# Layer 1 attention: each transpose of probabilities between two matmuls, its chain two steps later, ten tiles for probabilities

## Chip, cores and metric

The kernel runs on one core of a Trainium2 chip. The metric is the device time of one execution in microseconds, the median of three runs. The profile is of one further execution, taken by the hardware profiler; its instructions carry the line numbers of the kernel.

## What is computed

Two transformer layers on a batch of B = 4 sequences of S = 512 tokens with D = 512 features. Layer 0 is an attention with 32 heads of 16 features that share one key and value head, and a quantized linear layer. Layer 1 is an attention with 32 heads of 128 features over 8 key and value heads, with rotary positions, and a gated FFN with ternary weights. Each of the four parts adds a layer norm of its result to x. The part that the change is about, cut to its core:

```python
q = (hidden_states @ Wq.T).reshape(bsz, q_len, N_HEADS, HEAD_DIM).transpose(0, 2, 1, 3)
...
q = q * cos + _rotate_half(q) * sin
...
k = jnp.repeat(k, GROUPS, axis=1)
v = jnp.repeat(v, GROUPS, axis=1)
scale = 1.0 / jnp.sqrt(jnp.asarray(HEAD_DIM, dt))
scores = jnp.einsum('bhqd,bhkd->bhqk', q, k) * scale
causal = jnp.tril(jnp.ones((q_len, q_len), bool))
scores = jnp.where(causal[None, None], scores, jnp.asarray(-1000000000.0, dt))
attn = jax.nn.softmax(scores, axis=-1)
out = jnp.einsum('bhqk,bhkd->bhqd', attn, v)
out = out.transpose(0, 2, 1, 3).reshape(bsz, q_len, N_HEADS * HEAD_DIM)
return out @ Wo.T
```

All in float32. The shapes in the inputs make q_len 512.

## The kernel before

TensorE works here on operands rounded to a short float32 format. For float32 accuracy each operand is kept as a high and a low half, and a product is three matmuls: high by high, high by low, low by high (`mm3`, L182 to L184). A high half is a ScalarE copy, its low half a VectorE or GpSimd difference.

The program has three stages. Layer 0 and the key and value projections of layer 1 come first and end at about 760 us. Then comes layer 1's attention, `phase_b` (L859 to L1078), and then the FFN (`C.run`, L1169).

`phase_b` goes through 32 units u: 8 groups of four heads times 4 sequences. A unit has four blocks qb of 128 queries, and a block has four heads j. The loop of L1040 makes one step p for each (u, qb, j), so 512 steps and 12 more to drain. With G = p // 4, the number of the block, a step does:

- `score(u, qb, j)` (L954): two or three matmuls of 256 to 512 columns into one of three `psS` banks; VectorE adds the causal mask and finds the row's extreme in one pass (L966, L973); ScalarE takes exp (L977); VectorE a reciprocal (L979); GpSimd scales the row (L980). The result is a tile `s` of the pool `bs`, which has eight.
- `qproj` of the next unit at j = 1 (one head a block), `kproj` at the unit's fourth step: twelve matmuls into one of two `mm` banks, then `rope` (L847): VectorE L850, L852, L853, then GpSimd L854, ScalarE L855, GpSimd L856, through single tiles `rp_a` and `rp_b`.
- `trans(G - 1, kb = j)` (L986), if block G - 1 has a key block j: four transposes on TensorE (L989), one for each head, into one of two `psT` banks; ScalarE copies the bank to `ph` (L992), VectorE makes `pl` (L993).
- `pv` (L996) of the step before: three matmuls (L1002 to L1004) into the single `psO` bank; after the last key block ScalarE and VectorE make `oh` and `ol` (L1008, L1009), which free the bank.
- `oproj(G - 2)` (L1012) at j = 3: twelve matmuls into an `mm` bank, which VectorE adds to `acc`.

Weights come by `load_w` (L892): a DMA on GpSimd's queue into the high half, a second into the single tile `raw`, and a GpSimd difference `w_l` (L902). In the last unit the loop also advances `tail`, the FFN's front for sequence 0 (`C.front`, L1146): layer norms, and four transposes (L147) for each of four blocks of tokens, through one tile each of `x`, `an_t` and `xn` in the pool `cft`.

The order in each engine's queue isn't that of the calls. The framework's scheduler chooses, for every engine, among the instructions whose inputs its own timeline holds ready, and puts in the waits. `issue_after(a)` adds an edge: the instructions of its block come behind `a` on `a`'s engine.

Of the kernel before, what the change touches and what calls it, by code (L numbers as in the profile page):

```python
# [1 line left out]

# [1 line left out]

# [5 lines left out]
F32 = mybir.dt.float32  # L10
# [10 lines left out]
B, S, D = 4, 512, 512  # L21
# [837 lines left out]
def phase_b(tc, nc, c, aps, xt_d, wk_d, v_d, acc, xp, P, tern, tail):  # L859

    if True:
# [21 lines left out]
        nc.sync.dma_start(cosk, aps["c_cosk"])  # L883
        sink = cp.tile([128, S], F32, name="sink")
        nc.sync.dma_start(sink, aps["c_sink"])
        W = {}
        X = {}
        KV = {}
# [41 lines left out]
        def kproj(u):  # L930
            wh, wl = W["k", u // 4]
            xh, xl = X[u]
            ps = mmp.tile([128, S], F32, name="mm", tag="mm")
            mm3(nc, ps, lambda k: wh[:, bass.ts(k, 128)], lambda k: wl[:, bass.ts(k, 128)],
                lambda k: xh[:, k], lambda k: xl[:, k], range(KC))
            k = kvp.tile([128, 2, S], F32R, name="k", tag="k")
            rope(nc, tmp, k[:, 0], k[:, 1], ps, cosk, sink, nc.vector if u < 1 else nc.gpsimd)
            K[u] = k

        def qproj(u, j):  # L940
            h = 4 * (u // 4) + j
            wh, wl = W["q", h]
            xh, xl = X[u]
            ps = mmp.tile([128, S], F32, name="mm", tag="mm")
            mm3(nc, ps, lambda k: wh[:, bass.ts(k, 128)], lambda k: wl[:, bass.ts(k, 128)],
                lambda k: xh[:, k], lambda k: xl[:, k], range(KC))
            qh = qp.tile([128, S], F32R, name="qh", tag="qh")
            ql = qp.tile([128, S], F32R, name="ql", tag="ql")
            rope(nc, tmp, qh, ql, ps, cosq, sinq, nc.vector if u < 1 else nc.gpsimd)
            Q[u, j] = qh, ql  # L950

        PS = {}

        def score(u, qb, j):  # L954
            k = K[u]
            qh, ql = Q[u, j]
            nk = 128 * (qb + 1)
            ps = psS.tile([128, 512], F32, name="ps", tag="ps")
            qs = bass.ts(qb, 128)
            s = sp.tile([128, 512], F32, name="s", tag="s")  # L960
            mn = sm.tile([128, 1], F32, name="mn", tag="mn")
            if qb == 0:
                hl = ps.rearrange("p (i t) -> p i t", i=4)[:, 0:2]
                nc.tensor.matmul(hl, qh[:, qs], k[:, :, :nk], start=True, stop=False)
                nc.tensor.matmul(hl, ql[:, qs], k[:, :, :nk], start=False, stop=True)
                nc.vector.tensor_tensor(s[:, nk:2 * nk], ps[:, nk:2 * nk], c.mask[:, 384:512], ALU.add)  # L966
                mask = s[:, nk:2 * nk]
            else:
                nc.tensor.matmul(ps[:, :nk], qh[:, qs], k[:, 0, :nk], start=True, stop=False)  # L969
                nc.tensor.matmul(ps[:, :nk], qh[:, qs], k[:, 1, :nk], start=False, stop=False)  # L970
                nc.tensor.matmul(ps[:, :nk], ql[:, qs], k[:, 0, :nk], start=False, stop=True)  # L971
# [7 lines left out]
            nc.vector.reciprocal(r, l)  # L979
            nc.gpsimd.tensor_tensor(s[:, :nk], s[:, :nk], r.to_broadcast([128, nk]), ALU.mult)  # L980
            PS[u, qb, j] = s

        O = {}
        PT = {}

        def trans(u, qb, kb):  # L986
            pt = psT.tile([128, 4, 128], F32, name="pt", tag="pt")
            for j in range(4):
                nc.tensor.transpose(pt[:, j], PS[u, qb, j][:, bass.ts(kb, 128)], c.ident)  # L989
            ph = pp.tile([128, 4, 128], F32R, name="ph", tag="ph")  # L990
            pl = pp.tile([128, 4, 128], F32R, name="pl", tag="pl")
            nc.scalar.copy(ph, pt)  # L992
            nc.vector.tensor_tensor(pl, pt, f(ph), ALU.subtract)  # L993
            PT[u, qb, kb] = ph, pl

        def pv(u, qb, kb):  # L996
            vh, vl = KV[u]
            ph, pl = PT.pop((u, qb, kb))
            if kb == 0:
                O[u, qb] = psO.tile([128, 4, 128], F32, name="po", tag="po")  # L1000
            po = O[u, qb]
            nc.tensor.matmul(po, vh[:, kb], ph, start=(kb == 0), stop=False)  # L1002
            nc.tensor.matmul(po, vh[:, kb], pl, start=False, stop=False)  # L1003
            nc.tensor.matmul(po, vl[:, kb], ph, start=False, stop=(kb == qb))  # L1004
            if kb == qb:
                oh = op.tile([128, 4, 128], F32R, name="oh", tag="oh")
                ol = op.tile([128, 4, 128], F32R, name="ol", tag="ol")
                nc.scalar.copy(oh, po)  # L1008
                nc.vector.tensor_tensor(ol, po, f(oh), ALU.subtract)  # L1009
                O[u, qb] = oh, ol  # L1010

        def oproj(u, qb):  # L1012
            g, b = u // 4, u % 4
            oh, ol = O.pop((u, qb))
            y = mmp.tile([128, D], F32, name="mm", tag="mm")
            mm3(nc, y, lambda j: oh[:, j], lambda j: ol[:, j],
                lambda j: W["o", 4 * g + j][0], lambda j: W["o", 4 * g + j][1], range(4))
# [118 lines left out]
class C:  # L1136


    def __init__(self, tc, nc, c, aps, acc, x2_d, m_d, sc, out, xp, P):
        self.nc, self.c, self.acc, self.x2_d, self.m_d, self.sc, self.out = nc, c, acc, x2_d, m_d, sc, out  # L1140
        self.xp = xp
        self.ft = P(name="cft", bufs=1, side="right")
        self.sm = P(name="csm", bufs=3, side="right")
        self.X = {}

    def front(self, b):  # L1146
        mmp = self.c.mmp
        nc, c, sm = self.nc, self.c, self.sm
        xh = self.xp.tile([128, KC, S], F32R, name="xh", tag="xh")
        xl = self.xp.tile([128, KC, S], F32R, name="xl", tag="xl")  # L1150
        bank = Bank(mmp, "mm", Tok(1))
        for t in range(4):
            x = self.ft.tile([128, D], F32, name="x", tag="x")
            nc.sync.dma_start(x, self.x2_d[bass.ts(b * 4 + t, 128), :])
            a = self.acc[:, b * 4 + t]
            rs, nm = yield from ln_gen(nc, c, sm, a)
            tt = self.ft.tile([128, D], F32, name="an_t", tag="an_t")
# [4 lines left out]
            xn = self.ft.tile([128, D], F32, name="xn", tag="xn")  # L1162
            ln_apply(nc, xn, a, rs, nm)
            yield from hop(1)
            ts = bass.ts(t, 128)
# [80 lines left out]
def mega(tc, nc, aps, out):  # L1246
    with ExitStack() as top:
# [34 lines left out]
        with ExitStack() as e3:  # L1282
# [3 lines left out]
            pc = C(tc, nc, c, aps, acc, x2_d, m_d, sc, out, xp, P3)  # L1286
            with ExitStack() as eb:
                phase_b(tc, nc, c, aps, xt_d, wk_d, v_d, acc, xp, pools(eb), tern,
                        pc.front(0))
            with ExitStack() as ec:  # L1290
                pc.run(pools(ec))

# [94 lines left out]
```

## Time and profile before

| | |
|---|---|
| three runs | 2447.71, 2447.67, 2446.82 us; median 2447.67 |
| profiled execution | 2450.93 us, of which the span of its instructions is 2449.2 |
| TensorE matmul busy | 2314.0 us, 94% of the span |
| TensorE weight loads | 1801.1 us, 74%, beside matmuls |
| VectorE, GpSimd, ScalarE | 1574.3, 1202.1, 1075.2 us |
| DMA | 242.60 MB, mean 99 GB/s |
| L989, transposes of probabilities | 1280, 272 ns each in the mean, 212.6 us busy |
| L980, scaling on GpSimd | 512, 723 ns, 360.1 us busy |
| L992 and L993, `ph` and `pl` | 320 each, 586 and 686 ns |

Two things help to read it. Matmuls are pipelined: a matmul of 512 columns is recorded with some 0.39 us, but the next starts 0.23 us after it, so TensorE's pace is read from start to start and not from durations. And idle time of an engine that isn't the bottleneck costs nothing.

### The profile page before, as it was taken

To read this page: it belongs to the slowest core of one execution; us is meant where nothing else is said; L and a number is where in the kernel's file an instruction comes from. 1 tells how busy PE (TensorE), PEld (TensorE's weight loads), DVE (VectorE), ACT (ScalarE), POOL (GpSimd) and SP (SyncE) were. 2 spreads that over 40 slices of the span, in tenths; PEclk is the share of its full clock that TensorE was granted. 3 is DMA by queue.
4 is the path that set the end of the run, shared out by engine and by line. 5 is a ranking of instruction groups with operands and counts; after the bars stand their busy time and mean duration, and the time that the engine had idled before them with its cause. 6 is when DMAs were issued, how large, how long until landed. Compare 5 with 4: busy or idle time off the path is not lost.

```text
span 2449.2 us, 35859 instructions
## 1 busy us (share of the span) xinstructions
PE 2314.0 (94%) x11606; PEld 1801.1 (74%) x11606; DVE 1574.3 (64%) x4631; ACT 1075.2 (44%) x2400; POOL 1202.1 (49%) x1403
## 2 busy tenths in 40 slices
PE   6799889989976999999999999999999999999998
PEld 4566455655554788888888888888888888878887
DVE  7666566555343766777677677777767768764543
ACT  3555445445521444444444444444444445453332
POOL 3332333333342565666566566566666666631220
PEclk9899899999988999999999999999999999999999
DMA  8745434331338543231231232222232222042100
GB/s 180 234 145 177 97 88 109 98 104 60 106 104 237 128 134 104 78 117 58 78 124 63 97 104 91 74 87 104 76 103 72 84 98 74 18 102 75 34 27 18
DMA packets 155295, 242.60 MB, mean 99 GB/s; under 512 B 26802, under 2 KB 87474, under 8 KB 146276
## 3 DMA queue, kind: packets, MB, share of 16 engines
q1 hardware_dynamic: 136948, 199.27, 27.1%
q0 software_dynamic: 16304, 40.12, 5.8%
q8 instruction: 93, 1.52, 0.3%
q10 hardware_dynamic: 1856, 0.92, 0.2%
q14 instruction: 94, 0.77, 0.1%
HBM read 184.22 MB, written 63.92 MB: 101 GB/s over the span
## 4 chain that ended last, share of the span: by engine, by line
PE 82%; DMA 5%; issue 4%; DVE 3%; ACT 2%; POOL 2%; SPq 1%; ACTq 0%; POOLq 0%; DVEq 0%
PE mm L182 10%; PE mm L184 10%; PE mm L183 10%; PE pt L989 5%; PE mm L159 3%; PE po L482 3%; PE pt L466 3%; PE mm L161 3%; PE po L1003 3%; PE po L1002 3%; PE po L1004 3%; PE mm L160 3%; PE ps L969 3%; PE ps L971 3%; PE ps L970 3%
## 5 line engine op out<-in xcount | busy, mean ns | idle before, releaser
L980 POOL TENSOR_TENSOR s<-s,r 128x384 f32<-128x384 f32 (+3 forms) x512 | 360.1, 723 | 119.9 <-DVE r L979 110.4
L977 ACT ACTIVATE s<-s,mn 128x384 f32<-128x384 f32 (+3 forms) x512 | 286.0, 560 | 231.7 <-DVE mn L973 226.8
L854 POOL TENSOR_TENSOR rp_a<-rp_a,rp_b 128x512 f32<-128x512 f32 x155 | 200.7, 1295 | 273.4 <-DVE rp_b L853 264.4
L992 ACT CAST ph<-pt 128x512 fp32r<-128x512 f32 x320 | 181.9, 586 | 295.1 <-PE pt L989 292.7
L429 DVE CUSTOM_DVE_ANT_0 jk<-ps,mask 128x384 bf16<-128x384 f32 (+3 forms) x512 | 227.3, 483 | 82.0 <-PE ps L425 73.1
L993 DVE TENSOR_TENSOR pl<-pt,ph 128x512 fp32r<-128x512 f32 x320 | 216.4, 686 | 38.4 <-ACT ph L992 35.6
L973 DVE CUSTOM_DVE_ANT_0 s<-ps,mask 128x384 f32<-128x384 f32 (+2 forms) x384 | 203.1, 552 | 39.0 <-PE ps L971 19.1
L989 PE MATMUL pt<-ident,s 128*128 128x128 f32 x1280 | 212.6, 272 | 10.1 <-POOL s L980 9.9
L469 ACT ACTIVATE pe<-pt 128x512 f32<-128x512 f32 x307 | 174.6, 600 | 99.8 <-PE pt L466 95.7
L182 PE MATMUL mm<-xh,w_h 128*128 128x512 f32 x512 | 206.6, 403 | 5.5 <-DVE rp_b L853 5.5
L182 PE MATMUL mm<-w_h,oh 128*128 128x512 f32 x512 | 204.3, 399 | 2.6 <-DVE rp_b L853 1.9
L989 PEld LDWEIGHTS pt<-ident,s 128*128 128x128 f32 x1280 | 164.3, 140 | 55.3 <-POOL s L980 10.1
L184 PE MATMUL mm<-xh,w_l 128*128 128x512 f32 x512 | 204.4, 399 | 0.0
L183 PE MATMUL mm<-xl,w_h 128*128 128x512 f32 x512 | 202.9, 396 | 0.0
L183 PE MATMUL mm<-w_l,oh 128*128 128x512 f32 x512 | 202.0, 395 | 0.0
L184 PE MATMUL mm<-w_h,ol 128*128 128x512 f32 x512 | 201.0, 393 | 0.0
L856 POOL TENSOR_TENSOR ql<-rp_a,qh 128x512 fp32r<-128x512 f32 x124 | 160.6, 1295 | 45.2 <-ACT qh L855 45.1
L471 POOL TENSOR_SCALAR_AFFINE_SELECT pe<-pe 128x512 f32<-128x512 f32 x128 | 81.9, 642 | 200.1 <-ACT pe L469 198.7
L850 DVE TENSOR_TENSOR rp_a<-mm,cosq 128x512 f32<-128x512 f32 x128 | 88.4, 690 | 116.6 <-PE mm L184 87.3
L425 PE MATMUL ps<-KS,QS 128*128 128x256 f32 (+2 forms) x384 | 132.9, 384 | 19.2 <-DVE mn L429 18.6
L108 POOL TENSOR_TENSOR ln_rs<-ln_ve,mhalf 128x1 f32<-128x1 f32 x112 | 63.9, 577 | 169.7 <-DVE ln_ve L106 152.2
L1008 ACT CAST oh<-po 128x512 fp32r<-128x512 f32 x128 | 74.5, 582 | 154.8 <-PE po L1004 154.7
(338 smaller groups left out, 5896.9 us busy)
## 6 DMA issues: line engine op xcount, KB each, us to landing
xh<-xt SPq DMA_DIRECT2D x32, 1024.0 KB
xl<-xt SPq DMA_DIRECT2D x32, 1024.0 KB
v<-e_h SPq DMA_DIRECT2D x32, 256.0 KB
v<-e_l SPq DMA_DIRECT2D x32, 256.0 KB
raw<-in_a_wq SPq DMA_DIRECT2D x32, 256.0 KB
vh<-v SPq DMA_DIRECT2D x32, 256.0 KB
vl<-v SPq DMA_DIRECT2D x32, 256.0 KB
w_h<-in_a_wo POOLq DMA_DIRECT2D x32, 256.0 KB, 3.1
```

The source lines that it names most:

```text
L182: nc.tensor.matmul(ps, lh(k), rh(k), start=(j == 0), stop=False)
L183: nc.tensor.matmul(ps, lh(k), rl(k), start=False, stop=False)
L184: nc.tensor.matmul(ps, ll(k), rh(k), start=False, stop=(j == n - 1))
L429: nc.vector.tensor_tensor_reduce(out=jk[:, :nk], in0=p, in1=self.c.mask[:, 384 - 128 * qb:512], scale=-1.0, scalar=3e38, op0=ALU.add, op1= ...
L469: nc.scalar.activation(e, ps, AF.Exp)
L854: eng.tensor_tensor(a, a, r, ALU.add)
L973: nc.vector.tensor_tensor_reduce(out=s[:, :nk], in0=ps[:, :nk], in1=mask, scale=-1.0, scalar=3e38, op0=ALU.add, op1=ALU.min, accum_out=mn)
L977: nc.scalar.activation(s[:, :nk], s[:, :nk], AF.Exp, bias=mn, scale=-1.0, accum_out=l)
L980: nc.gpsimd.tensor_tensor(s[:, :nk], s[:, :nk], r.to_broadcast([128, nk]), ALU.mult)
L989: nc.tensor.transpose(pt[:, j], PS[u, qb, j][:, bass.ts(kb, 128)], c.ident)
L992: nc.scalar.copy(ph, pt)
L993: nc.vector.tensor_tensor(pl, pt, f(ph), ALU.subtract)
```

## The change

- `trans` issues nothing itself any more. It puts its four transposes into a list `pend`. All matmuls of `phase_b` go through `mm`, which issues its matmul behind the transpose that was issued last (`behind`), and then one transpose from the list behind that matmul. So as long as the list holds transposes, a matmul and a transpose take turns, and edges hold them in that order; where it is empty there are no edges. With the fourth transpose `split_p` makes `ph` and `pl`. `pv` empties the list first if its `ph` and `pl` aren't there yet.
- `trans` is called ahead of `score` in its step, and two steps later (`LAG = 2`); `pv` and `oproj` follow it. The loop has two steps more.
- The pool `bs` has ten tiles instead of eight. The pool `cft` goes from beside `phase_b`; the FFN's front for sequence 0 takes its tiles from `bs`, and the later fronts from a pool of three tiles that the FFN opens.

```diff
-        sp = P(name="bs", bufs=8)
+        sp = P(name="bs", bufs=10)
...
+        pend = []
+        behind = []
+        def tick():
+            if pend:
+                behind[:] = [pend.pop(0)()]
+        def mm(*a, **k):
+            with tc.issue_after(behind.pop().ins) if behind else nullcontext():
+                ins = nc.tensor.matmul(*a, **k)
+            if pend:
+                with tc.issue_after(ins.ins):
+                    tick()
...
         def trans(u, qb, kb):
             pt = psT.tile([128, 4, 128], F32, name="pt", tag="pt")
-            for j in range(4):
-                nc.tensor.transpose(pt[:, j], PS[u, qb, j][:, bass.ts(kb, 128)], c.ident)
+            def one(j):
+                ins = nc.tensor.transpose(pt[:, j], PS[u, qb, j][:, bass.ts(kb, 128)], c.ident)
+                if j == 3:
+                    split_p(u, qb, kb, pt)
+                return ins
+            pend.extend(partial(one, j) for j in range(4))
+        def split_p(u, qb, kb, pt):
             ph = pp.tile([128, 4, 128], F32R, name="ph", tag="ph")
...
         def pv(u, qb, kb):
             vh, vl = KV[u]
+            while (u, qb, kb) not in PT:
+                tick()
             ph, pl = PT.pop((u, qb, kb))
...
+        LAG = 2
...
-        for p in range(NU * 16 + 12):
+        for p in range(NU * 16 + 12 + LAG):
             G, j = p // 4, p % 4
             u, qb = G // 4, G % 4
+            G1, j1 = (p - LAG) // 4 - 1, (p - LAG) % 4
...
-                    tg = tail
+                    tg = tail.front(0, sp)
                 next(tg, None)
+            todo, pvq = pvq, []
+            if 0 <= G1 < NU * 4 and j1 <= G1 % 4:
+                trans(G1 // 4, G1 % 4, j1)
+                pvq.append((G1 // 4, G1 % 4, j1))
             if u < NU:
                 score(u, qb, j)
...
-            todo, pvq = pvq, []
-            G1 = G - 1
-            if 0 <= G1 < NU * 4 and j <= G1 % 4:
-                trans(G1 // 4, G1 % 4, j)
-                pvq.append((G1 // 4, G1 % 4, j))
             for t in todo:
                 pv(*t)
-            G2 = G - 2
-            if j == 3 and 0 <= G2 < NU * 4:
+            G2 = G1 - 1
+            if j1 == 3 and 0 <= G2 < NU * 4:
                 oproj(G2 // 4, G2 % 4)
...
-        self.ft = P(name="cft", bufs=1, side="right")
...
-    def front(self, b):
+    def front(self, b, pool):
+        new = lambda name: pool.tile([128, D], F32, name=name, tag="s")
...
-            x = self.ft.tile([128, D], F32, name="x", tag="x")
+            x = new("x")
...
+        ftp = P(name="cft", bufs=3)
...
-            fr = self.front(b + 1) if b + 1 < B else iter(())
+            fr = self.front(b + 1, ftp) if b + 1 < B else iter(())
```

All other matmuls of `phase_b` are rewritten from `nc.tensor.matmul` and `mm3(nc, ...)` to `mm` and a local `mm3` that calls it, with the same operands in the same order.

More of the change, by code (lines that the diff above doesn't have):

```diff
@@ L1 @@
 from contextlib import ExitStack, nullcontext
+from functools import partial
 import numpy as np
@@ L885, in phase_b, with mm3 @@
         nc.sync.dma_start(sink, aps["c_sink"])
+        pend = []
[9 more added lines that the diff above has]
+                    tick()
+        def mm3(ps, lh, ll, rh, rl, ks):
+            n = len(ks)
+            for j, k in enumerate(ks):
+                mm(ps, lh(k), rh(k), start=(j == 0), stop=False)
+                mm(ps, lh(k), rl(k), start=False, stop=False)
+                mm(ps, ll(k), rh(k), start=False, stop=(j == n - 1))
         W = {}
@@ L963, in score @@
                 hl = ps.rearrange("p (i t) -> p i t", i=4)[:, 0:2]
-                nc.tensor.matmul(hl, qh[:, qs], k[:, :, :nk], start=True, stop=False)
-                nc.tensor.matmul(hl, ql[:, qs], k[:, :, :nk], start=False, stop=True)
+                mm(hl, qh[:, qs], k[:, :, :nk], start=True, stop=False)
+                mm(hl, ql[:, qs], k[:, :, :nk], start=False, stop=True)
                 nc.vector.tensor_tensor(s[:, nk:2 * nk], ps[:, nk:2 * nk], c.mask[:, 384:512], ALU.add)
@@ L968, in score @@
             else:
-                nc.tensor.matmul(ps[:, :nk], qh[:, qs], k[:, 0, :nk], start=True, stop=False)
-                nc.tensor.matmul(ps[:, :nk], qh[:, qs], k[:, 1, :nk], start=False, stop=False)
-                nc.tensor.matmul(ps[:, :nk], ql[:, qs], k[:, 0, :nk], start=False, stop=True)
+                mm(ps[:, :nk], qh[:, qs], k[:, 0, :nk], start=True, stop=False)
+                mm(ps[:, :nk], qh[:, qs], k[:, 1, :nk], start=False, stop=False)
+                mm(ps[:, :nk], ql[:, qs], k[:, 0, :nk], start=False, stop=True)
                 mask = c.mask[:, 384 - 128 * qb:512]
@@ L1001, in pv @@
             po = O[u, qb]
-            nc.tensor.matmul(po, vh[:, kb], ph, start=(kb == 0), stop=False)
-            nc.tensor.matmul(po, vh[:, kb], pl, start=False, stop=False)
-            nc.tensor.matmul(po, vl[:, kb], ph, start=False, stop=(kb == qb))
+            mm(po, vh[:, kb], ph, start=(kb == 0), stop=False)
+            mm(po, vh[:, kb], pl, start=False, stop=False)
+            mm(po, vl[:, kb], ph, start=False, stop=(kb == qb))
             if kb == qb:
@@ L1015, in oproj @@
             y = mmp.tile([128, D], F32, name="mm", tag="mm")
-            mm3(nc, y, lambda j: oh[:, j], lambda j: ol[:, j],
+            mm3(y, lambda j: oh[:, j], lambda j: ol[:, j],
                 lambda j: W["o", 4 * g + j][0], lambda j: W["o", 4 * g + j][1], range(4))
@@ L1156, in front @@
             rs, nm = yield from ln_gen(nc, c, sm, a)
-            tt = self.ft.tile([128, D], F32, name="an_t", tag="an_t")
+            tt = new("an_t")
             nc.scalar.activation(tt, a, AF.Identity, bias=nm, scale=rs)
@@ L1161, in front @@
             rs, nm = yield from ln_gen(nc, c, sm, a)
-            xn = self.ft.tile([128, D], F32, name="xn", tag="xn")
+            xn = new("xn")
             ln_apply(nc, xn, a, rs, nm)
@@ L1288, in mega @@
                 phase_b(tc, nc, c, aps, xt_d, wk_d, v_d, acc, xp, pools(eb), tern,
-                        pc.front(0))
+                        pc)
             with ExitStack() as ec:
```

4 lines of the change are left out of this document (2 added, 2 removed).

## Prediction

> **What bounds the kernel now.** I read the page's 40 slices first, then busy time by stretch (columns: TensorE, its weight loads, VectorE, ScalarE, GpSimd, clock), then the instructions in order of time.
>
> ```profile
> PE   6799889989976999999999999999999999999998
> ...
> POOL 3332333333342565666566566566666666631220
> PEclk9899899999988999999999999999999999999999
> ```
>
> ```profile
> 1200.00:1400.00 200.00, 200.00 (x1018) 167.16 (x1017) 143.69 (x387) 89.99 (x231) 125.13 (x137) 1.00 0.25 82
> ```
>
> Layer 1's attention runs from about 763 to 2190 us. After its first 60 us TensorE is busy without a break at full clock, while VectorE has 144 of 200 us, ScalarE 90 and GpSimd 125. A busy TensorE can still hide a short wait, because its matmuls overlap, so I added up start-to-start times. Between 830 and 2100 us a 512-column matmul takes 231 ns from its start to the next one's, 384 columns 175, 256 columns 118. With those and 110 ns per transpose, the sum of the work and the trace's clock drift apart by 2.1 us at 888 us (a wait for a free `mm` bank) and by some 1.5 us in all the rest. So the middle has no waits to win. What is left to win is at its start: from 780 to 823 us the trace falls 18.6 us behind the sum. The tail, 2100 to 2194, falls 6.4 behind.
>
> **1. What a lone transpose costs.** The timeline of TensorE (start and duration in us, engine, line, operation; in brackets the idle time before and what ended it) has both shapes, a run of four and single ones:
>
> ```profile
> 1200.23 0.60 PE L989 MATMUL pt<-ident,s 128*128 128x128 f32 x4
> 1200.59 0.37 PE L970 MATMUL ps<-k,qh 128*128 128x256 f32 x1
> 1200.79 0.40 PE L1002 MATMUL po<-ph,vh 128*128 128x512 f32 x1
> ...
> 1205.27 0.27 PE L989 MATMUL pt<-ident,s 128*128 128x128 f32 x1
> 1205.29 0.42 PE L969 MATMUL ps<-k,qh 128*128 128x384 f32 x1
> 1205.55 0.34 PE L970 MATMUL ps<-k,qh 128*128 128x384 f32 x1
> 1205.73 0.34 PE L971 MATMUL ps<-k,ql 128*128 128x384 f32 x1
> ```
>
> The lone transpose is left after 20 ns, but the matmul behind it then takes 1205.55 - 1205.29 = 260 ns where an undisturbed one of 384 columns takes 175. Together that is 105 to 112 ns. The four take 1200.79 - 1200.23 = 560 ns less the 118 of the matmul that follows: 442, or 110 each. Over 830 to 2100 us the 77 lone ones cost 111.8 ns on average, the 164 runs of four 110.5 each, and no length of run is cheaper than 109. Where one matmul stood between two lone transposes (7 cases), it was 114.3. So whoever comes after a transpose pays for a weight load that 128 columns can't cover, be it the next transpose or a matmul. In the changed program's order 1270 of 1280 transposes stand alone (before: 448 runs). I take 112.5 against 110.4: 1280 x 2.1 ns = **+2.7 us**; the ends are 0 and 3.9 x 1280 = 5 us.
>
> [...]
>
> **2. Waits that the order brings in.** Each transpose now hangs on the matmul before it, and the next matmul on it, so the scheduler can no longer put ready matmuls between a group's last transpose and its use. The chain behind a transpose is: ScalarE's copy `ph`, VectorE's `pl`, then the matmuls of L1002 to L1004. At the end of the layer the trace shows it bare:
>
> ```profile
> 2181.77 0.60 PE L989 MATMUL pt<-ident,s 128*128 128x128 f32 x4
> ...
> 2182.46 0.59 ACT L992 CAST ph<-pt 128x512 fp32r<-128x512 f32 x1 [1.37 <-PE pt L989]
> ...
> 2183.70 0.67 DVE L993 TENSOR_TENSOR pl<-pt,ph 128x512 fp32r<-128x512 f32 x1
> ...
> 2184.42 0.50 PE L1003 MATMUL po<-pl,vh 128*128 128x512 f32 x1 [0.82 <-DVE pl L993]
> ```
>
> TensorE starts 0.05 us after `pl` ends (2183.70 + 0.67 = 2184.37). In the middle of the layer, from the start of a group's last transpose, `ph` ends after 0.90 us at the least (median 1.12), `pl` after 1.62 (lower quartile 1.85, median 2.47). Against that I hold the work that the two programs put on TensorE between that transpose and its users, in the durations above. Before, the least is 2.41 us to the user of `ph` and 3.00 to that of `pl`, and no wait is seen. After, the order repeats from head group to head group, and:
>
> - At 30 places (about one in each of 32 units of four heads) `pl` has 1.72 to 1.84 us. Needed are 1.67 with both engines free, 1.90 at the quartile, 2.52 at the median: a wait of 0, 0.2 or 0.8. VectorE's queue at this place holds one small mask addition of a score (0.29 us) just ahead of `pl`. Laying the rows' durations end to end in queue order, `pl` ends 0.05 to 0.4 us late. I take 0.2: 30 x 0.2 = **+6 us** (0 to 24).
> - At 6 places, in the units that also load new weights, `ph` has 0.34 us and needs 0.95: 6 x 0.65 = **+3.9 us** (2 to 5).
> - At 7 places a score's bank is wanted again after 1.15 us. At 1.57 the trace shows no wait; I take 0 (up to 5, at 0.7 each, one 0.68 reduction of a score being in the way).
>
> Behind a waiting matmul stands all of TensorE, whose idleness is the layer's time; the other engines catch up meanwhile, so waits don't add to each other's price.
>
> **3. The start of the layer.** Here the lag of two steps and ten tiles work:
>
> ```profile
> 784.46 0.28 PE L965 MATMUL ps<-k,ql 128*128 128x256 f32 x1
> 794.68 0.47 PE L989 MATMUL pt<-ident,s 128*128 128x128 f32 x1 [9.94 <-POOL s L980]
> ```
>
> ```profile
> 801.45 1.31 POOL L902 TENSOR_TENSOR w_l<-raw,w_h 128x512 fp32r<-128x512 f32 x1 [6.46 <-DMA raw<-in_a_wo]
> 803.46 0.40 POOL L980 TENSOR_TENSOR s<-s,r 128x128 f32<-128x128 f32 x1 [0.70 <-DVE r L979]
> 805.51 1.30 POOL L854 TENSOR_TENSOR rp_a<-rp_a,rp_b 128x512 f32<-128x512 f32 x1 [1.65 <-DVE rp_b L853]
> ```
>
> The first transpose holds TensorE for 10.2 us, since GpSimd's queue has four `w_l` differences ahead of the scaled scores, each behind a DMA into the single `raw` tile. The clock then falls: the next matmuls take 427 ns, 2.6 us lost in all. After the change the first transpose stands behind 12.9 us of work instead of 3.3, so this wait goes. What is late next? GpSimd keeps its order, and its fourth `w_l` still ends at 801.45 + 1.31 = 802.76. Behind it are one scaling (0.40) and the first rope addition of unit 1, then at about 803.2 where it was 805.51. Every following projection needs an `mm` bank, which a rope frees, and ropes go one after another through the single `rp_a`: VectorE 2.07, GpSimd 1.30, ScalarE 0.62, GpSimd 1.30. The last big wait of the start before (819.78 to 822.23, for VectorE's `rp_b`) is the end of that chain, so it moves by the 2.3 us that the chain starts earlier, and the 10 us are mostly given back there. I take **-2 us**; the ends are 0 and -12.8 (10.2 + 2.6).
>
> **4. The tail.** The two extra steps put the last transposes and the last four L1002 to L1004 groups closer together. `po` has one bank: before, 2.01 us of other work lay between its last two owners (0.43 us of wait); after, 0.23, where the copy `oh` (0.58), `ol` (0.69) and 0.25 of drain must pass. About 1.3 of wait replaces 0.43: **+1 us** (-2, if the front of the FFN gains by its shared tiles, to +3).
>
> **The rest.** The FFN's front for batch 0 takes its three tiles from the ten of the scores, and the later ones from a pool of three in place of three of one each: the same rotation, hidden under the FFN's matmuls; 0 (up to 2 where a score waits for a tile). Output projections move by two steps; their `oh`, `ol` and bank come in time by the order (1.2 us at the least before, 2.2 after). Loads are issued at the same steps on SP's and GpSimd's queues. In layer 0, which no edit touches, the scheduler also gives another order of the same matmuls (1043 of 2916 positions). TensorE idles 120 of the first 800 us; I let a thirtieth of that go either way: 0, +-4 us.
>
> **Sum:** 2.7 + 6 + 3.9 + 0 - 2 + 1 + 0 = +11.6 us. The profiled execution took 2450.93 (span 2449.2 and 1.7 around it), so 2462.5; against the median of the three runs, 2447.67, which is 3.3 lower, it is **2459**. About 0.2%, 4.9 us, is what a measurement of this kernel can tell from no change.
>
> **Rivals.**
> - *The new waits vanish* (25%): ScalarE and VectorE are free at the 30 places and `pl` comes in 1.67. What remains is 2.7 + 3.9 - 2 + 1 = +5.6, or +1.7 without the six: 2449 to 2453. For it: no wait in the middle before. Against: 1.62 is the least of 314 groups, and half of them take over 2.47.
> - *Faster by the start* (15%): the wait for GpSimd at 784 is 12.8 us with its slow clock. If the fourth `raw` lands earlier than 801 us, or the scheduler's order lets ropes pass, the 12.8 stay won: 2447.67 - 12.8 + 2.7 + 1 = 2439, with the waits of part 2 gone, 2443 with the six left. It decides as soon as those cost less than some 4 us. Against: the rope chain above.
> - *The median, not the quartile* (13%): queues at the 30 places are as full as usual, 0.8 each: 24 + 3.9 + 2.7 + 1.4 + 1 - 2 = +31, 2479.
> [...]
>
> **How the numbers follow.** The forecast has 46%, with 2453 to 2468 as its own range. Faster: 15 + 1 = 16%. Within 0.2%: 25%. Slower: 46 + 13 = 59%. The range reaches down to 2440, so that half of the fast case is in, and up to 2475, below the median case: some 80%.
>
> **What would show it.** Right: lone transposes at 110 to 114 ns with the next matmul's; in the waits of TensorE a row of some 10 us for `pl` and `ph`, in equal steps from 870 to 2130 us; the first transpose without its wait, but waits for `rp_b` up to 820. Wrong: no idle TensorE in the middle; the layer's first unit done 10 us sooner; or a matmul behind a lone transpose at its undisturbed time.

## The result and the profile after

The changed kernel takes 2477.47 us in the median of four runs (2474.38 to 2480.60), the kernel before 2447.69 beside it: a ratio of 1.0122 (95% interval 1.0105 to 1.0140). It is 29.8 us slower; I had forecast 11 and a range that ends at 2475. Measured once more in another session, the same program took 2472.76 us, a ratio of 1.0110 (1.0094 to 1.0126). The profiled execution took 2479.49 us, with a span of 2477.8.

The 40 slices of the page show nothing of it, and the table of busy times for 1200 to 1400 us shows little (columns as before):

```profile
PE   6799889989976999999999999999999999999998
...
POOL 3323333333442665665665666565665656522220
PEclk8899999999988999999999999999999999999999
```

```profile
1200.00:1400.00 200.00, 197.96 (x996) 163.04 (x995) 143.84 (x381) 92.05 (x230) 124.58 (x136) 1.00 0.25 80
```

TensorE was busy for all of the 200 us before and is for 197.96 now, with some twenty matmuls fewer. The waits of TensorE from 870 to 2130 us (what waited, for which engine's tile; us in all, times, longest) name the waits that are long enough to leave it idle:

```profile
PE pt L1015 <- POOL s L1005: 6.7, 6, 1.6
PE po L899 <- ACT ph L1025: 3.0, 6, 0.5
PE mm L899 <- DVE rp_b L854: 2.7, 1, 2.7
PE po L899 <- DVE pl L1026: 0.2, 1, 0.2
```

The `ph` row was in the forecast, the first one wasn't, and of a row for `pl` there is next to nothing.

To see where each microsecond went I take, as in the prediction, the clock's time less the sum of the work, with the same durations (231, 175.5 and 118.5 ns for matmuls of 512, 384 and 256 columns, 110 for a transpose), from the layer's first score on. All kernels below have the same work, 1383.5 us up to the FFN's first matmul, so the same marks can be put in each: 68, 150 and 1310 us of work, which is about 860, 945 and 2100 to 2145 us of the clock. "Behind" is what a stretch takes more than its work.

| kernel | median us | ratio (95%) | first score at | behind: start, to 68 | 68 to 150 | middle, 150 to 1310 | tail |
|---|---|---|---|---|---|---|---|
| before | 2447.67 | 1 | 780.0 | 19.1 | 2.3 | 1.3 | 5.8 |
| changed | 2477.47 | 1.0122 | 778.7 | 16.4 | 5.5 | 22.1 | 14.9 |
| after_again: changed, once more | 2472.76 | 1.0110 (1.0094-1.0126) | 772.2 | 18.2 | 2.9 | 22.4 | 15.0 |
| e1_together: no turns | 2436.29 | 0.9960 (0.9945-0.9975) | 771.9 | 16.8 | 2.0 | 0.9 | 3.0 |
| e1_confirm: the same again | 2438.19 | 0.9964 (0.9951-0.9977) | 769.7 | 16.8 | 1.0 | 1.0 | 2.9 |
| e6_no_edges: turns, no edges | 2441.90 | 0.9982 (0.9972-0.9993) | 772.9 | 17.0 | 4.9 | 2.7 | 3.5 |
| e2_tiles_only: before, ten tiles | 2442.18 | 0.9984 (0.9971-0.9996) | 772.4 | 15.8 | 1.1 | 2.6 | 4.4 |
| e3_lag0: turns without the lag | 2493.18 | 1.0184 (1.0165-1.0204) | 776.3 | 17.3 | 4.4 | 35.7 | 17.8 |
| e4_tail_together: no turns in the last unit | 2464.65 | 1.0075 (1.0057-1.0094) | 774.3 | 16.6 | 7.0 | 20.8 | 6.2 |
| f2_spread_wl: output weights spread | 2467.73 | 1.0088 (1.0072-1.0104) | 777.4 | 17.2 | 2.2 | 13.3 | 14.5 |
| f3_pv_later: `pv` a step later | 2456.74 | 1.0042 (1.0027-1.0058) | 773.8 | 21.6 | 0.9 | 4.1 | 11.6 |
| e5_raw2: two `raw` tiles | 2469.97 | 1.0098 (1.0082-1.0114) | 776.1 | 9.6 | 17.7 | 8.8 | 15.1 |
| e7_together_raw2: no turns, two `raw` | 2446.54 | 0.9997 (0.9987-1.0008) | 778.0 | 13.7 | 10.8 | 0.7 | 2.9 |
| f1_together_late_wl | 2443.02 | 0.9983 (0.9974-0.9993) | 775.4 | 23.9 | 0.0 | 1.5 | 2.9 |

Profiles are of one execution each, so a row's stretches needn't add up to its median (e2_tiles_only's profiled execution took 2438.10, e1_confirm's 2433.26). The kernel before had medians of 2446.2 to 2446.4 beside the later ones. The first score, whose code ahead no edit touches, comes at 778.7 and at 772.2 us for one and the same program: some 7 us of any single comparison are not the change's. So stretches are compared from the first score on.

Between the two profiles of the first session the sum closes: first score -1.3, start -2.7, 68 to 150 +3.2, middle +20.8, tail +9.1, FFN -0.6: +28.5, and the spans differ by 28.6. **The loss is made in the middle and in the tail.**

**The middle, +20.8.** At six places, in the units that load new weights, a transpose waits for a score that GpSimd hasn't scaled yet. TensorE at one of them (start, duration, operation; idle time before and its cause in brackets), and GpSimd at the same time:

```profile
1279.57 0.28 PE L899 MATMUL ps<-k,qh 128*128 128x256 f32 x1
1281.40 0.33 PE L1015 MATMUL pt<-ident,s 128*128 128x128 f32 x1 [1.55 <-POOL s L1005]
```

```profile
1272.58 1.30 POOL L927 TENSOR_TENSOR w_l<-raw,w_h 128x512 fp32r<-128x512 f32 x1 [0.43 <-PE ps L899]
1277.83 1.29 POOL L927 TENSOR_TENSOR w_l<-raw,w_h 128x512 fp32r<-128x512 f32 x1 [3.95 <-DMA raw<-in_a_wo]
1279.08 1.27 POOL L855 TENSOR_TENSOR rp_a<-rp_a,rp_b 128x512 f32<-128x512 f32 x1
1280.31 1.75 POOL L1005 TENSOR_TENSOR s<-s,r 128x512 f32<-128x512 f32 x3
```

The second `w_l` waits 3.95 us for its load, because the one `raw` tile is free only when the first `w_l` has read it, at 1273.88; SP's queue issues the load just then:

```profile
1273.90 5.58 SPq L925 DMA_DIRECT2D raw<-in_a_wo  x2
```

Three scalings stand behind the second `w_l`. In the kernel before GpSimd does the same work here in another order, with three scalings ahead of the `w_l`:

```profile
1274.56 1.12 POOL L980 TENSOR_TENSOR s<-s,r 128x128 f32<-128x128 f32 x3 [1.10 <-DVE r L979]
1275.75 1.30 POOL L902 TENSOR_TENSOR w_l<-raw,w_h 128x512 fp32r<-128x512 f32 x1
```

From start to start the six waits cost 7.6 us (0.26 to 1.71 each), and the restarts behind them 1.0 more. At six other places `ph` is late; TensorE shows 0.49 idle, and 0.66 from start to start, 3.95 in all and 0.75 for the restarts:

```profile
1009.52 0.48 PE L899 MATMUL po<-ph,vl 128*128 128x512 f32 x1
1010.49 0.50 PE L899 MATMUL po<-ph,vh 128*128 128x512 f32 x1 [0.49 <-ACT ph L1025]
```

At 27 places, one in nearly every unit, `pl` comes just in time for the matmul, but not for its weight load. TensorE's weight loads at one of them:

```profile
971.54 0.19 PEld L899 LDWEIGHTS po<-pl,vh 128*128 128x128 f32 x1 [0.26 <-DVE pl L1026]
971.65 0.19 PEld L899 LDWEIGHTS po<-ph,vl 128*128 128x128 f32 x1
```

The load of the waiting matmul shows 0.26 us of idle time put down to `pl`, though the 128x128 that it reads are of `vh`. `pl` ends at 971.49, and load and matmul both start at 971.54; the load ahead of it starts at 971.08, 0.24 us before its matmul at 971.32. The next matmul starts at 971.88, after 0.34 us instead of 0.23. That is 0.10 at each, 2.8 us in all, and no idle time is shown. Two further waits for `pl`, at 2079 and 2081 us, are 0.8 together. Waits above 45 ns come to 16.8 us (before: 0.5). The other 4.5 us of the 20.8 lie in pieces below 45 ns. A kernel below that has the lone transposes and almost no waits shows 3.0 us of this; what the remaining 1.5 are isn't shown.

**The tail, +9.1.** TensorE just before the layer's end:

```profile
2200.53 0.39 PE L899 MATMUL po<-ph,vl 128*128 128x512 f32 x1
2202.32 0.80 PE L899 MATMUL po<-ph,vh 128*128 128x512 f32 x1 [1.40 <-DVE ol L1044]
...
2204.20 0.63 PE L1015 MATMUL pt<-ident,s 128*128 128x128 f32 x2
2205.55 0.80 PE L899 MATMUL po<-ph,vh 128*128 128x512 f32 x1 [0.73 <-ACT ph L1025]
```

The wait for the single `po` bank is there as forecast (1.56 us from start to start, through `oh` and `ol`). What is new is that the last groups' transposes, with edges between them and the few matmuls that are left, have nothing to stand before the user of `ph`: 1.12 us twice. And the matmuls take 0.80 where they took 0.39: the granted clock was 0.51 from 2202 to 2212 us. By my estimate that costs some 3.6 us: 11 matmuls at 0.43 us instead of 0.23, a twelfth at 0.39, and 12 transposes at 0.21 instead of 0.11. The kernel before has such a stretch too, from 2186.3 to 2189.7 us, with a granted clock of 0.50, where a matmul takes 0.43 us from start to start instead of 0.23. It costs some 1.5, estimated from the 3.36 us between 2186.45 and 2189.81 less 1.83 of work (six matmuls at 231 ns, four transposes at 110):

```profile
2185.83 0.50 PE L182 MATMUL mm<-w_h,oh 128*128 128x512 f32 x1 [0.68 <-ACT oh L1008]
...
2188.16 0.63 PE L183 MATMUL mm<-w_l,oh 128*128 128x512 f32 x1
2188.59 0.63 PE L184 MATMUL mm<-w_h,ol 128*128 128x512 f32 x1
```

So some 2 of the 9.1 us are a slower clock by these two estimates, and nearly all the rest is waits.

In the changed kernel the granted clock falls from 1.00 to 0.50 at 2202.2 us, 1.28 us into the gap of 1.40, and 1.8 of the 3.0 us up to there, from the first gap's start at 2199.18, were idle. In the kernel before it falls to 0.50 at 2186.3, the longest gap ahead of the fall is 0.82 us, and 1.5 of the 2.7 us from that gap's start at 2183.60 were idle.

### The profile page after: what moved, and what is told of

Read it like the earlier page. It is cut to its first block, busy times and chain, and to the rows that moved or that the text cites. A ratio compares the mean times of both kernels' runs of the same rounds, so it can differ in the third digit from the quotient of the medians.

```text
span 2477.8 us, 35648 instructions
## 1 busy us (share of the span) xinstructions
PE 2330.3 (94%) x11606; PEld 1793.9 (72%) x11606; DVE 1597.6 (64%) x4631; ACT 1097.5 (44%) x2400; POOL 1201.5 (48%) x1403
## 4 chain that ended last, share of the span: by engine, by line
PE 80%; DMA 5%; DVE 5%; issue 4%; ACT 2%; POOL 2%; SPq 2%; ACTq 0%; POOLq 0%; DVEq 0%
PE mm L899 30%; PE ps L899 9%; PE po L899 9%; PE pt L1015 5%; PE mm L160 3%; PE po L483 3%; PE pt L467 3%; PE mm L162 3%; PE mm L161 3%; PE ps L426 3%; PE gu L1238 3%; PE gu L1239 3%; SPq L1166 1%; PE mm L1256 1%; PE mm L1257 1%
## 5 line engine op out<-in xcount | busy, mean ns | idle before, releaser
L1015 PE MATMUL pt<-ident,s 128*128 128x128 f32 x1280 | 336.5, 273 | 9.6 <-POOL s L1005 9.5
L1025 ACT CAST ph<-pt 128x512 fp32r<-128x512 f32 x320 | 187.3, 586 | 323.5 <-PE pt L1015 321.3
L899 PE MATMUL ps<-k,qh 128*128 128x256 f32 (+2 forms) x896 | 277.3, 364 | 0.0
L998 DVE CUSTOM_DVE_ANT_0 s<-ps,mask 128x384 f32<-128x384 f32 (+2 forms) x384 | 209.5, 553 | 52.8 <-PE ps L899 50.3
L1015 PEld LDWEIGHTS pt<-ident,s 128*128 128x128 f32 x1280 | 180.0, 141 | 28.6 <-POOL s L1005 11.7
L899 PEld LDWEIGHTS ps<-k,qh 128*128 128x128 f32 x896 | 163.5, 189 | 35.8
L899 PE MATMUL ps<-k,ql 128*128 128x256 f32 (+2 forms) x512 | 187.7, 375 | 0.0
L856 ACT CAST qh<-rp_a 128x512 fp32r<-128x512 f32 x128 | 79.3, 620 | 215.9 <-POOL rp_a L855 193.5
```

The costliest lines, as they stand in the source:

```text
L899: ins = nc.tensor.matmul(*a, **k)
L998: nc.vector.tensor_tensor_reduce(out=s[:, :nk], in0=ps[:, :nk], in1=mask, scale=-1.0, scalar=3e38, op0=ALU.add, op1=ALU.min, accum_out=mn)
L1015: ins = nc.tensor.transpose(pt[:, j], PS[u, qb, j][:, bass.ts(kb, 128)], c.ident)
```

## The experiments

Main theory after the result: turns held by edges forbid the scheduler to fill between a group's transposes and their users, and they shift GpSimd's order; lag and tiles do no harm. Rivals: the lag itself; the tiles and the front; lone transposes as such; the single `raw` tile.

**e1_together**: all of the change but the turns.

```diff
-            pend.extend(partial(one, j) for j in range(4))
+            for j in range(4):
+                one(j)
```

> The changed kernel with its lag of two steps and its ten tiles, but a group's four transposes issued at once and no edges. Main theory (the order with a matmul between transposes brings the new waits in the middle, 16.8 us, and 8.2 in the tail, while lag and tiles help the start by 2.7): the waits on GpSimd's scaling, on ph and pl in the middle go, the tail falls back to some 7 us, the start gain stays; 2440 to 2449 us. Rival 1 (the lag itself costs: two steps more at the end and a GpSimd that is behind whatever the order of transposes): 2455 to 2470, with the six waits on GpSimd still there. Rival 2 (ten tiles and the shared front cost): above 2455, and the second kernel of this batch, which has only these, slower too.

2436.29 us, 0.9960 (0.9945 to 0.9975): faster than both kernels, and 4 us below the range that I gave. The middle falls from 22.1 to 0.9 behind and the tail to 3.0, below the 5.8 of the kernel before. Rival 1 falls: the two extra steps don't lengthen the end. Against the changed kernel on the same first score (771.9 and 772.2) turns and edges cost 58.5 - 22.7 = 35.8 us; the medians differ by 36.5. The start's wait for GpSimd is still there, 9.0 us at the first transpose, though lag and tiles are those of the changed kernel:

```profile
PE pt L1015 <- POOL s L1005: 10.8, 3, 9.0
```

In TensorE's order 3.2 us of work stand ahead of that transpose, as in the kernel before, and 12.9 in the changed one (9.3 in e3_lag0 below, which has turns and edges without the lag). So turns and edges moved it; the lag alone moves nothing there.

**e2_tiles_only**: the kernel before with ten tiles and the front's tiles taken from them, LAG and turns left out.

> The kernel before with ten tiles in place of eight and the front's tiles taken from them; transposes, lag and order of calls as before. Main theory: tiles neither help nor harm much, 2443 to 2451 us, the first transpose still waits for GpSimd's scaling with some 10 us. Rival 2 (tiles or the shared front cost): above 2455, with scores or the front waiting for tiles. Rival 3 (the start gain comes from the tiles and not from the lag): the wait of 9.9 us shrinks below 5.

2442.18 us, 0.9984 (0.9971 to 0.9996). Rival 2 falls. The wait of the first transpose is 8.9 us as expected, so rival 3 falls too by the sign that I gave it. But the start is 15.8 behind with tiles alone, 3.3 less than in the kernel before, so it isn't shown that the start's gain needs the lag. How much of the gain in the first kernel is the lag's and how much the tiles', I can't say: their intervals overlap, and in the stretches they differ by 1 to 2 us.

**e4_tail_together**: the changed kernel, with no turns in the last unit.

```diff
+            if u == NU - 1:
+                while pend:
+                    tick()
+                for j in range(4):
+                    one(j)
+                return
```

> The changed kernel, but in the last of the 32 units each group's four transposes are issued at once, so that the tail has the order of the kernel before with two steps more. Main theory (the tail's 8.2 us come from the turn-taking there: waits on ph, oh and ol behind edges, and the half clock that follows them): 2469 to 2473 us, the offset of the tail back to some 7 us, no slice at half clock after 2202 us. Rival 1 (the two extra steps themselves): the tail stays within 2 us of 14.9, 2476 to 2480.

2464.65 us, 8.1 below the changed kernel of the later session, and 4 below the range that I gave, which started from the first session's 2477. The tail goes from 15.0 to 6.2 behind; the granted clock is 1.00 from 2190 to 2208 us. The turns and their edges make the tail's loss.

**e5_raw2**: the changed kernel with two `raw` tiles.

```diff
-        raws = P(name="braw", bufs=1)
+        raws = P(name="braw", bufs=2)
```

> The changed kernel with two tiles in place of one for raw, the landing place of a weight's second copy, and nothing else. Theory: the six waits of TensorE on GpSimd's scaling (7.6 us, about 1 us more behind them) come from a w_l difference that waits for its DMA at the head of GpSimd's queue (3.95 us at 1277 us), because the one raw tile lets the next DMA start only when the difference before it is done; with two tiles the DMA is early and these waits go: 2462 to 2469 us, and the start (three such waits before 802 us) a few us shorter. Rival (GpSimd is late at these units from work and not from the DMA, or the DMA is late for another reason): the six waits stay within a third, 2474 to 2480.

2469.97 us, 1 us above the range. In the middle the theory holds: no wait for GpSimd is left, waits above 45 ns fall from 17.0 to 3.9 us (the ones for `ph` go too, since the order moves), and the start is 9.6 behind instead of 18.2. But one new wait of 12.3 us at 902 takes most of it back. GpSimd's queue and SP's around it:

```profile
892.44 1.60 POOL L1005 TENSOR_TENSOR s<-s,r 128x384 f32<-128x384 f32 x2
912.50 1.26 POOL L927 TENSOR_TENSOR w_l<-raw,w_h 128x512 fp32r<-128x512 f32 x1 [18.45 <-DMA raw<-in_a_wo]
```

```profile
902.25 7.40 SPq L1166 DMA_DIRECT2D m_d<-t_d  x10
909.75 0.43 SPq L925 DMA_DIRECT2D raw<-in_a_wo  x1
```

GpSimd stands 18.45 us at a `w_l` whose load is issued only at 909.75, behind ten copies of the FFN's weights (`m_d<-t_d`) on SP's queue.

**after_again**: the changed kernel unaltered.

> The changed kernel once more, unaltered, so that it stands on the same chip as the other kernels of this batch. Its first measurement (2474.4 to 2480.6 in four runs, ratio 1.0122) and the variants of the first batch came from different chips' sessions, and the first score of the layer began at 778.7 us there and at 771.9 to 776.1 in the variants. If layer 0 is only the chip's clock, the first score comes at 772 to 776 here and the ratio is 1.009 to 1.012; if it is the order of layer 0, it stays at 778 to 779 and the ratio at 1.0122. In the middle (950 to 2130 us) the same 16 to 18 us of waits are expected either way.

2472.76 us; the first score at 772.2 us, so its late place wasn't the program's. Whether it was the session's or the single execution's, one profile of each can't tell. Middle and tail come out within 0.3 us of the first profile.

**e3_lag0**: the changed kernel with `LAG = 0`.

> The changed kernel with its edges, single transposes and ten tiles, but without the lag (LAG = 0). Theory: the lag is what the turn-taking order needs, because a block's scaled scores must be there when its transposes are at the head of TensorE's queue; without it the least work between a score and its transpose falls from some 12 to 7.6 us, and waits on GpSimd's scaling come in every unit: 2485 to 2530 us, with over 15 us of waits on GpSimd in the middle. Rival (the lag does nothing in the middle, only ph and pl count): within 8 us of the changed kernel.

2493.18 us, 1.0184 (1.0165 to 1.0204); the middle is 35.7 behind. The waits of TensorE from 950 to 2095 us have one large row:

```profile
PE pt L1015 <- POOL s L1005: 13.7, 29, 0.8
```

That is idle time; from start to start the waits come to 31.4 us, 24 of them ahead of a transpose. So the lag saves the turns some 20 us (2493.18 - 2472.76): it hides VectorE, ScalarE and GpSimd between score and transpose. The lag covers part of what the turns cost.

**e6_no_edges**: turns in the calls, no edges.

```diff
-            with tc.issue_after(behind.pop().ins) if behind else nullcontext():
-                ins = nc.tensor.matmul(*a, **k)
-            if pend:
-                with tc.issue_after(ins.ins):
-                    tick()
+            nc.tensor.matmul(*a, **k)
+            tick()
```

> The changed kernel with the calls in turns (a transpose called after every matmul) but without the edges, so that the scheduler may put ready matmuls in between; runs of single transposes are 393 and of four 104 in its order, and ph has at least 1.49 us of work before its user, pl 4.96. Main theory (the edges, which forbid to fill, cause the waits on ph, pl and GpSimd, not the single transposes as such): middle waits under 3 us, 2437 to 2448 us. Rival (calling transposes one by one is enough to bring the waits): over 10 us of waits in the middle, 2462 to 2480.

2441.90 us, 0.9982 (0.9972 to 0.9993); 1.1 us of waits in the middle. The edges alone account for 58.5 - 28.1 = 30.4 us of the changed kernel's time. The scheduler, left free, regroups the transposes (in the middle 343 of 1064 stand alone, in the changed kernel all) and fills.

**f2_spread_wl**: the changed kernel, each output-weight load in a block of its own, its `w_l` behind a scaling.

```diff
-                if p % 16 == 12:
-                    for jj in range(4):
-                        load_w("o", u // 4 + 1, jj)
+                if p % 4 == 0:
+                    load_w("o", u // 4 + 1, qb)
...
+            with tc.issue_after(SC[0].ins) if which == "o" and SC else nullcontext():
+                eng.tensor_tensor(wl, raw, f(wh), ALU.subtract)
...
+            SC[:] = [nc.gpsimd.tensor_tensor(s[:, :nk], s[:, :nk], r.to_broadcast([128, nk]), ALU.mult)]
```

> The changed kernel with its edges on TensorE, and the loads of output weights spread: in the units that load weights one head's load in each block instead of four at one step, and each w_l held by an edge behind a scaling of its time on GpSimd's queue. Nothing on TensorE is changed. Theory: the six waits of TensorE on GpSimd's scaling (7.8 us on this chip, 1.1 us more behind them) come from two w_l that stand ahead of the scalings on GpSimd's queue while their loads into the one raw tile land; spread, each load has a block's time and these waits go: 2462 to 2467 us, middle waits from 17.0 to 7 to 9. Rival (GpSimd has too much to do at these units however it is ordered): the six waits stay above 5 us, 2469 to 2475.

2467.73 us, 0.7 above the range, with a first score 5 us later than in after_again. The waits in the middle are 8.2 us (expected 7 to 9), the six for GpSimd are gone, `ph` and `pl` stay within 0.05 us. GpSimd at the unit shown above:

```profile
1277.46 0.40 POOL L1007 TENSOR_TENSOR s<-s,r 128x128 f32<-128x128 f32 x1 [0.21 <-DVE r L1006]
1278.22 0.40 POOL L1007 TENSOR_TENSOR s<-s,r 128x128 f32<-128x128 f32 x1 [0.36 <-DVE r L1006]
1278.58 1.29 POOL L929 TENSOR_TENSOR w_l<-raw,w_h 128x512 fp32r<-128x512 f32 x1
```

The scalings pass, and the `w_l` finds its load there. TensorE's order is that of the changed kernel up to each of the six waiting transposes; behind each, one score matmul moves by 17 places. So the six waits were GpSimd's queue and nothing else.

**f3_pv_later**: the changed kernel with `pv` a step later, four tiles of `ph` and `pl`, and nine of the probabilities, as they need the room.

```diff
-            todo, pvq = pvq, []
+            todo, pvq, pvq2 = pvq2, [], pvq
```

> The changed kernel with its edges, but pv a step later, so that more work lies between a group's last transpose and the users of ph and pl; ph and pl get four tiles each instead of three, and to fit them the probabilities nine instead of ten. By the order the least work ahead of ph's user goes from 0.23 to 1.39 us, and ahead of pl's from 1.61 to 2.08. Theory: the six waits on ph (3.95 us) and most of the 27 small ones at pl (2.8 us) go, the six on GpSimd's scaling stay, the tail stays long: middle waits from 17.0 to 9 to 11 us, 2463 to 2471 us. Rival (nine tiles are too few with this order, or users wait whatever the distance): middle waits above 14 us, 2472 or more.

2456.74 us, better than I expected: waits above 45 ns in the middle are 0.3 us, not 9 to 11. `ph` and `pl` went as expected; the six on GpSimd went too, which this theory had staying. In the new order the `w_l` stand between scalings, and the one at 1275 us waits 1.09 us for its load instead of 3.95. So the six waits belong to the place of `w_l` in GpSimd's queue, which this change of order moved. The middle's 4.1 us behind, less 0.3 of waits, are 3.8, against 0.8 in the kernel before: 3.0 us is what the 1073 transposes of the middle, all alone, cost without waits, some 2.8 ns each. The tail stays at 11.6.

**e7_together_raw2** and **f1_together_late_wl** try to better the first kernel at its start. The first has two `raw` tiles; the second holds the four `w_l` of the first output weights behind the scalings of block 0.

> The first kernel of the first batch (lag 2, ten tiles, four transposes at once, 2436.3 us there) with two raw tiles. Theory: its largest stall, the 9.0 us of the first transposes waiting for GpSimd's scaling at 776 us, comes from the w_l differences that wait for raw ahead of it; with two tiles the loads come earlier: 2427 to 2434 us. Rival (the scheduler puts a w_l on GpSimd's queue ahead of scalings while its load still stands on SP's queue behind other transfers, as it did at 902 us with two tiles in the changed kernel, 12.3 us): 2436 to 2448, with a new wait of 8 to 13 us between 860 and 960 us.

2446.54 us, 0.9997 (0.9987 to 1.0008): no gain, and the rival's wait is there, 10.8 us behind between 68 and 150 us of work.

> Lag 2, ten tiles and four transposes at once (the first kernel of the first batch, 2436.3 us), and the four w_l differences of the first output weights held behind the scalings of block 0, one after every second step, by edges on GpSimd's queue alone; their loads may still start early. Theory: the first transposes wait 9.0 us and 1.8 us for GpSimd's scaling (776 to 795 us) only because these w_l, each behind its load into the one raw tile, stand ahead of it; then these waits go and what is late next is the rope chain (rp_b), as in the prediction: start offset from 16.8 to 8 to 12 us, 2427 to 2433 us, 0.992 to 0.995 of the kernel before. Rival (something else holds GpSimd, or the rope chain takes all of it back, as my prediction had for the start): start offset within 2 us of 16.8, 2434 to 2439.

2443.02 us, 0.9983 (0.9974 to 0.9993), so slower than the kernel it was to better (2438.19 beside it). The start is 23.9 behind, outside both expectations. The first scalings do pass, at 779 us, but the next load of `raw` comes later still, on SP's queue and then on GpSimd's:

```profile
788.75 15.15 SPq L1169 DMA_DIRECT2D m_d<-t_d  x19
804.00 0.52 SPq L926 DMA_DIRECT2D raw<-in_a_wo  x1
```

```profile
806.98 1.26 POOL L929 TENSOR_TENSOR w_l<-raw,w_h 128x512 fp32r<-128x512 f32 x1 [10.88 <-DMA raw<-in_a_wo]
```

The `raw` tile was free at 793.12, when the `w_l` ahead had read it, but on SP's queue 19 copies stood ahead of the load. In the kernel before, copies hold only the first two of these four loads. The third and fourth are issued within 0.03 us of the tile's release, and from the fourth's issue at 794.30 to its `w_l` at 801.45 it takes 7.15 us, where the other three take 2.84 to 3.04. So the start has more than one limit: the queue, the single tile and a slow landing. Moving `raw` to another queue wasn't tried.

**e1_confirm**: the first kernel once more.

> The first kernel of the first batch once more, unaltered, in five rounds, beside the kernels of this batch: lag 2, ten tiles, a group's four transposes at once. It had 2436.3 us and 0.996 (0.9945 to 0.9975) in four runs, while its first score of the layer and that of another kernel differ by up to 8 us between sessions. If it is faster than the kernel before, the ratio is 0.995 to 0.998 again, with an interval that leaves out 1; if the first result was the session's, 0.999 to 1.001.

2438.19 us, 0.9964 (0.9951 to 0.9977). It is the best version found, 0.36% below the kernel before and 34.6 us below the changed one.

## Why the prediction was wrong, by its steps

The sign was right and for the reason given, new waits by a rigid order. The size was less than half of what came.

- *Lone transposes, +2.7:* right, as far as it is shown. The kernel without other waits (f3_pv_later) has 3.0 in the middle. The changed kernel has 4.5 there beside its waits, of which 1.5 stay open. The weight load that I named as what the next matmul pays for has its row in the kernel before: it starts at 1205.27, with the lone transpose, and takes 0.19 us, and its matmul takes 0.26 instead of 0.175. The 1 in the chance of faster, 15 + 1, was for a next matmul at its undisturbed time. No run shows that: at 969.84 us in the changed kernel one of 512 columns behind a lone transpose takes 0.32 from start to start, where an undisturbed one takes 0.23.
- *`ph` at six places, +3.9:* right, 3.95 and 0.75 for the restarts, which I hadn't priced.
- *`pl` at 30 places, +6:* 27 places, 2.8 us. The places and the nearness were right; the size 0.2 was 0.10. `pl` came in time for the matmul, and only the weight load was late.
- *Score banks at seven places, 0:* right, no wait there.
- *"Loads are issued at the same steps on SP's and GpSimd's queues", cost 0:* **this step failed**, by 8.6 us with the restarts. I counted distances on TensorE only from the transpose on, and gave the way from a score through GpSimd's queue to its transpose no price. The calls stand at the same steps, but the scheduler orders GpSimd's queue anew, and two `w_l` with a load between them came ahead of the scalings. A queue in which one instruction waits for a DMA has to be followed in the new order, however long the distance.
- *Start, -2:* the first transpose lost its wait of 10.1 us, as forecast, but by the turns and edges, and not by lag and tiles alone (e1_together has both and waits 9.0). The third and fourth transposes still wait 3.1 us for GpSimd, waits for `rp_b` grow from 5.2 to 8.3, and one of 1.8 for `pl` is new: -2.7 in all. But 3.2 us come back at 912 us, in another wait for `rp_b`, of 2.68 us, with a granted clock of 0.50 behind it from 915.4 to 918.6 us. In the second profile it is -0.9 and +0.6. The net is nothing.
- *Tail, +1:* **this step failed too**: +9.1. I priced the two extra steps and the `po` bank, but not the edges, which are the same as in the middle and find even less to stand between. e1_together has the two steps and gains 2.8 against the kernel before; e4_tail_together takes the edges out of the last unit and gains 8.8 against the changed one. The last wait for the `po` bank, which I had put down to the two steps, is 1.56 us with the edges and 0.21 in e4_tail_together, which has the steps as well. Some 2 us are the clock (0.51 from 2202 to 2212 us), which I had priced at the start of the layer and not here.
- *Layer 0, 0 +-4:* too narrow: one program differs from itself by 6.5 us there.

The rival of the full queues had 2479 us, near the result, but by 0.8 us at each of the 30 places; these gave 0.10. It was near by accident. Its term of 1.4 has no working either.

## What to carry to other kernels

An edge that fixes the order on the busiest engine takes away the scheduler's freedom to cover latencies; price it by the chain behind each fixed instruction, at the tail too, where nothing is left to fill with. And follow every other queue in the new order: here the six places where scalings stood behind a `w_l` on GpSimd's queue, which at 1277 us waited 3.95 us for its DMA, cost 8.6 us with the restarts, about as much as all the waits that the distances on TensorE showed (4.7 for `ph`, 3.6 for `pl`). When a change bundles an order with the slack that it needs (a lag, more tiles), try the slack alone.

## What the runs showed of the hardware

- At 27 places of the changed kernel the weight load of the matmul that uses `pl` starts within 0.01 us of that matmul, with 0.26 to 0.28 us of idle time put down to `pl`. At the place shown, the load ahead of it starts 0.24 us before its own matmul. The next matmul then starts after 0.33 to 0.34 us instead of 0.23, and the profile shows no idle matmul time.
- In the changed kernel the granted clock fell from 1.00 to 0.50 after 1.8 us of idle time within 3.0, and stayed there for 10 us, while two waits of 0.73 us followed. In the kernel before it fell to 0.50 after 1.5 us within 2.7, no gap over 0.82, and stayed for 3.4.
- One and the same program reached the layer's first score at 778.7 us in one session and at 772.2 in another; the program of e1_together and e1_confirm at 771.9 and 769.7.
